# One pool of eight PSUM banks for a fused cross-attention and FFN layer: scores merged into three stretches a step

## The chip, the cores and the metric

The kernel runs on one core of a Trainium2 chip. The metric is device time in microseconds (us) of one launch. The engines are TensorE (PE), VectorE (DVE), ScalarE (ACT), GpSimd (POOL) and SyncE (SP), which issues the DMAs.

## The reference

For 32 batches of 224 tokens (`x`, width 512) and 750 context rows (width 384), a gated cross-attention is followed by a gated feed-forward network whose two linear layers are quantised:

```python
x = x + tanh(g_xattn) * attention(layernorm(x), ctx, mask, Wq, Wkv)     # 16 heads of 32
x = x + tanh(g_ffn)   * ffn(layernorm(x), w1, b1, w2, b2)               # 512 -> 2048 -> 512
# attention: q = x Wq^T, (k, v) = ctx Wkv^T; where(mask, q k^T / sqrt(32), -1e9); softmax; times v
# ffn: two layers, each on rmsnorm'ed tokens rounded to 8 bits with one scale a token and ternary weights;
#      an exact gelu lies between them
```

## The kernel before, in words

Attention is worked in 128 **steps**: 32 batches times 4 groups of 4 heads (`steps`). Four heads of width 32 fill the 128 rows of TensorE. In a step `n` the kernel does two things with scores.

- `maxima(b, g, i)`, for `i` in 0 to 2, computes the scores of step `n + 1` in the layout tokens by keys (matmuls `sm`, 112 rows) and DVE takes row maxima of them (`mx<-sm`). After `i == 2`, `minus_max` splits the negated maximum into three bf16 parts (six small DVE reductions), and `turn_max` turns them on TensorE (`pn`), with an ACT copy to `nT`.
- `weights(b, g, u)`, for `u` in 0 to 2, computes the scores of step `n` in the layout keys by tokens (matmuls `se`: first `nT` against ones, then keys against queries), and ACT takes `Exp` of all 1792 columns in one instruction (`p<-se`). POOL adds the results up into `acc`.

Both kinds of scores use one PSUM tile of four banks (`ps_s`, one buffer), in turn. Each step so has six **slots**: an even slot begins with `maxima` of the next step, an odd slot with `weights` of this step.

After the scores of a slot come **fillers**, which are matmul groups with an eviction each: `pk` (keys, evicted by ACT to `kT`), `pv` (values, by ACT or DVE to `v`), `pq` (queries, by DVE to `qT`), `pn`, `values` and `sums` (the weighted sums `po`, turned out by DVE to `oT`), and of the FFN `ph` (first layer, by DVE to `h`) and `po2` (second layer, `po` in the profile, by DVE to `xg`). Every filler takes a tile of its own from `ps_m`, a pool of four buffers of one bank each, so that a matmul waits only for the eviction of the filler that was four before it.

The order on each engine is the order of the program text (`Ordered` keeps it), and the framework puts in the semaphore waits, from the tiles that instructions write and read. `put(k, us, fn)` assigns a unit to a slot; units marked `first` come before the FFN's. `Ffn.fill` then draws FFN units as long as their estimated PE, ACT and DVE time fits the slot's room (`PE_ROOM`, less what is assigned), and the slot's other units follow. `Ffn.drain` writes out what is left after the last step, by a list of estimated durations. In the first steps `weight_units` quantises the FFN weights.

The names of the profile's groups are tiles: `sm` and `se` are scores, `p` the exponentials, and all instructions carry line 53, the line of the recording helper.

## Time and profile before

| | |
|---|---|
| three runs | 2985.87, 2986.15, 2988.3 us; median 2986.15 |
| span of the profiled execution, first to last instruction | 2983.6 us; its own time lies about 2.5 us above by the median run |
| PE busy | 2892.7 us (97%) |
| DVE, ACT, POOL busy | 1737.2, 1414.2, 2084.4 us (58%, 47%, 70%) |
| mean granted TensorE clock | 0.993 |
| HBM | 119.74 MB read, 29.27 MB written |
| first `se` matmul, first `se` of the last step, end | 32.9, 2894.9, 2983.6 us |

The profile has no separate time for the profiled execution beside its span, so the median run is set beside the span. The page gives busy shares and a chain of the work that ended last; the answers of the trace give groups of instructions, waits, a timeline in order of time, and windows. PE's rows are matmuls, PEld's the weight loads that run beside them. Ends of matmuls are modelled, so starts are the safer reading.

### The profile page before, as it was taken

How to read it: one execution, taken by the hardware profiler on the slowest of the kernel's cores; microseconds unless marked ns; L12 is line 12 of the kernel's file. 1: busy time of each engine (PE TensorE's matmuls, PEld its weight loads, DVE VectorE, ACT ScalarE, POOL GpSimd, SP SyncE). 2: the span in 40 equal slices, each digit the busy share in tenths (PEclk: the TensorE clock that was granted, in tenths of full speed). 3: DMA queues.
4: the chain of work that ended last, by engine and by line, in shares of the span. 5: the costliest groups of instructions: out<-in, count | busy, mean ns of one | idle time of the engine just before them, and what ended most of it. 6: DMA issues, size and time to landing. Idle time of an engine off the chain costs nothing.

```text
span 2983.6 us, 62984 instructions
## 1 busy us (share of the span) xinstructions
PE 2892.7 (97%) x26814; PEld 1840.7 (62%) x26814; DVE 1737.2 (58%) x2616; ACT 1414.2 (47%) x1438; POOL 2084.4 (70%) x2723
## 2 busy tenths in 40 slices
PE   8999999999999999999999999999999999999985
PEld 5666566666666666666666666666666666666653
DVE  5566555555556565555555565655655655556556
ACT  2344454544545455445445454544544554545444
POOL 3566767767766876777667777767767777777675
PEclk9999999999999999999999999999999999999998
DMA  5433222223222222222232212123122132222123
GB/s 148 106 99 98 55 50 73 43 62 75 42 61 61 52 55 73 69 44 48 63 73 47 65 40 80 48 62 74 45 50 62 45 71 67 50 71 48 39 52 78
DMA packets 375785, 189.80 MB, mean 64 GB/s; under 512 B 282160, under 2 KB 339920, under 8 KB 375376
## 3 DMA queue, kind: packets, MB, share of 16 engines
q1 hardware_dynamic: 375504, 185.79, 25.6%
q8 instruction: 209, 3.42, 0.5%
q14 instruction: 72, 0.59, 0.1%
HBM read 119.74 MB, written 29.27 MB: 50 GB/s over the span
## 4 chain that ended last, share of the span: by engine, by line
PE 82%; ACT 10%; POOL 3%; DVE 2%; issue 1%; DMA 1%; POOLq 0%; SPq 0%; ACTq 0%; DVEq 0%
PE po L53 17%; PE pk L53 15%; PE se L53 14%; PE sm L53 13%; PE pv_None L53 8%; ACT p L53 7%; PE pv L53 6%; PE ph L53 6%; PE pq L53 3%; DVE mx L53 2%; ACT L53 2%; POOL acc L53 1%; ACT h L53 1%; PE pn L53 1%; POOL h L53 1%
## 5 line engine op out<-in xcount | busy, mean ns | idle before, releaser
L53 POOL TENSOR_TENSOR acc<-acc,p 125x896 f32<-125x896 f32 x510 | 1066.9, 2092 | 324.8 <-ACT p L53 303.6
L53 DVE TENSOR_REDUCE mx<-sm 112x4 f32<-112x2000 f32 (+1 forms) x384 | 861.2, 2243 | 669.3 <-PE sm L53 669.2
L53 ACT ACTIVATE p<-se 125x1792 f32<-125x1792 f32 x384 | 638.8, 1663 | 760.6 <-PE se L53 706.9
L53 PE MATMUL pk<-y,wkv_sb 128*128 128x375 f32 x1536 | 541.6, 488 | 1.5 <-DMA y<-in_ctxT 1.5
L53 PE MATMUL sm<-kT,qT 32*112 32x500 f32 (+1 forms) x4096 | 426.9, 508 | 31.6 <-ACT p L53 22.7
L53 POOL TENSOR_TENSOR acc<-p 125x896 f32<-125x896 f32 x128 | 268.3, 2096 | 240.3 <-ACT p L53 237.1
L53 PEld LDWEIGHTS pk<-y,wkv_sb 128*128 128x128 f32 x1536 | 279.2, 190 | 175.7 <-issue 36.9
L53 PE MATMUL se<-qT,kT 32*125 32x224 f32 x6144 | 359.9, 348 | 0.0
L53 PE MATMUL po<-p,v 125*32 125x224 f32 x6144 | 317.1, 354 | 0.0
L53 PE MATMUL pv<-wkv_sb,y 128*125 128x256 f32 x1248 | 311.0, 385 | 0.0
L53 PEld LDWEIGHTS se<-qT,kT 32*125 32x125 f32 x6144 | 295.4, 183 | 0.1
L53 PEld LDWEIGHTS sm<-kT,qT 32*112 32x112 f32 x4096 | 159.3, 170 | 190.6 <-ACT p L53 137.6
L53 PEld LDWEIGHTS po<-p,v 125*32 125x32 f32 x6144 | 186.5, 110 | 118.9 <-issue 43.1
L53 PEld LDWEIGHTS pv<-wkv_sb,y 128*125 128x125 f32 x1248 | 223.3, 188 | 52.3 <-issue 17.8
L53 ACT COPY kT<-pk 128x375 f32<-128x375 f32 x256 | 120.1, 469 | 282.0 <-PE pk L53 281.2
L53 PE MATMUL pv_None<-wkv_sb,y 128*125 128x256 f32 x1056 | 250.9, 387 | 0.0
L53 PEld LDWEIGHTS pv_None<-wkv_sb,y 128*125 128x125 f32 x1056 | 191.3, 187 | 88.9 <-issue 59.7
L53 PE MATMUL po<-w2q,hT 128*128 128x256 fp8e4 x1792 | 220.9, 279 | 20.8 <-DMA hT<-hq 20.7
L53 DVE SCALAR_TENSOR_TENSOR h<-ph,qa_am,b_sb 128x512 f32<-128x512 f32 x216 | 158.5, 745 | 137.8 <-PE ph L53 110.3
L53 PE MATMUL ph<-w1q,xT 128*128 128x512 fp8e4 x896 | 224.9, 382 | 6.5 <-DMA xT<-xc 4.2
L53 PE MATMUL pq<-xTb,wq_sb 128*128 128x224 f32 x1024 | 221.4, 359 | 0.4 <-DVE wq_sb L53 0.4
L53 PEld LDWEIGHTS <-hT 128*128 128x128 bf16 x1792 | 171.5, 100 | 72.3 <-issue 27.1
(147 smaller groups left out, 2875.1 us busy)
## 6 DMA issues: line engine op xcount, KB each, us to landing
y<-in_ctxT SPq DMA_DIRECT2D x90, 375.0 KB, 4.4
x<-in_x SPq DMA_DIRECT2D x32, 448.0 KB, 4.1
xTb<-in_xT SPq DMA_DIRECT2D x32, 448.0 KB, 3.7
o_d<-yo SPq DMA_DIRECT2D x508, 28.0 KB, 1.8
xg<-in_x SPq DMA_DIRECT2D x26, 512.0 KB, 3.7
og<-o_d SPq DMA_DIRECT2D x26, 512.0 KB, 4.4
out<-xg SPq DMA_DIRECT2D x52, 256.0 KB, 2.1
wa<-in_w1T SPq DMA_DIRECT2D x8, 512.0 KB, 3.8
```

Source lines behind the costliest of these rows:

```text
L53: return lambda *args, **kw: tc.keep_in_program_order(build(*args, **kw))
```

## The change

The two pools in PSUM become two tiles of four banks, `s_lo` and `s_hi`. `weights` always writes `s_lo` and `maxima` always `s_hi`. The fillers take banks of these same tiles from `bank()`: after `take_banks(LOW + HIGH, HIGH)` the first four fillers of a stretch get the banks of `s_lo` in order, and further ones those of `s_hi`.

A step has three stretches: `weights`, at once `maxima`, then the fillers of two of the old slots. The maxima run a stretch ahead: the first third of step `n + 2` is already done in the last stretch of step `n`, and `turn_max` of step `n + 1` there too. The weighted sums of the step before move from slot 2 to the end of slot 1, the second `pk` from slot 1 to slot 2, and the `pq` of `g > 1` are put before the `pv` of their slots. The exponential is taken in two instructions of two banks each. The rooms for FFN units are set anew.

```diff
-    ps_s = pool("ps_s", 1, PSUM)
-    ps_m = pool("ps_m", 4, PSUM)
+    ps = pool("ps", 1, PSUM)
+    NB = 8
+    LOW, HIGH = list(range(NB // 2)), list(range(NB // 2, NB))
+    s_lo = ps.tile([P, NB // 2, 512], F32, name="s_lo")
+    s_hi = ps.tile([P, NB // 2, 512], F32, name="s_hi")
+    turn_of = {"order": LOW, "again": LOW, "at": 0}
+    def take_banks(order, again):
+        turn_of.update(order=order, again=again, at=0)
+    def bank():
+        n, order, again = turn_of["at"], turn_of["order"], turn_of["again"]
+        turn_of["at"] += 1
+        i = order[n] if n < len(order) else again[(n - len(order)) % len(again)]
+        return (s_lo if i < NB // 2 else s_hi)[:, i % (NB // 2), :]
...
-            pk = ps_m.tile([P, 512], F32, tag="m", name=f"pk_{b}_{g}_{half}")
+            pk = bank()
...
-        s = ps_s.tile([P, HG, 512], F32, tag="s", name=f"sm_{b}_{g}_{i}")
+        s = s_hi
...
-        s = ps_s.tile([P, HG, 512], F32, tag="s", name=f"se_{b}_{g}_{u}")
+        s = s_lo
...
-        act.activation(p.rearrange("p j i n -> p j (i n)"), s[:KC, :, : 2 * S], AF.Exp)
+        for two in (slice(0, HG // 2), slice(HG // 2, HG)):
+            act.activation(
+                p[:, two].rearrange("p j i n -> p j (i n)"), s[:KC, two, : 2 * S], AF.Exp
+            )
...
-    PE_ROOM = 2.5, 1.9
+    PE_ROOM = 5.2, 3.0
...
-        put(0, 0.2, lambda: turn_max(n), first=True)
+        put(4, 0.2, lambda: turn_max(n + 1), first=True)
         if last:
-            put(2, 2.7, lambda: (values(*last), sums(*last)), first=True)
-            put(5, 0.0, lambda: store(*last), first=True)
+            put(4, 0.0, lambda: store(*last), first=True)
...
+        if last:
+            put(1, 2.9, lambda: (values(*last), sums(*last)))
         for k in range(6):
             if k % 2 == 0:
-                maxima(*nxt, k // 2)
-            else:
-                if k == 3 and last:
+                take_banks(LOW + HIGH, HIGH)
+                if k == 2 and last:
                     finish(*last)
                 weights(b, g, k // 2)
-            if k == 4:
-                minus_max(n + 1)
+                at, i = ahead[k // 2]
+                if at < N:
+                    maxima(*steps[at], i)
+                if i == 2:
+                    minus_max(at)
+                room = PE_ROOM[0] - sum(us for us, _ in slots[k] + slots[k + 1])
...
+    take_banks(HIGH, HIGH)
     last = steps[-2:]
```

Here `ahead = [(n + 1, 1), (n + 1, 2), (n + 2, 0)]`.

More of the change, by code (lines that the diff above doesn't have):

```diff
@@ L209, in centre @@
     def centre(lo, hi):
-        pw = ps_m.tile([P, 512], F32, tag="m", name=f"pwq_{lo}")
+        pw = bank()
         for c in range(NDC):
@@ L246, in spread @@
             if b == 0:
-                pr = ps_m.tile([P, NQ, CP], F32, tag="m", name="prb")
+                pr = bank()[:, : NQ * CP].rearrange("p (t n) -> p t n", t=NQ)
                 for t in range(NQ):
@@ L262, in q_piece @@
         def q_piece(g, between=None):
-            pq = ps_m.tile([P, 512], F32, tag="m", name=f"pq_{b}_{g}")
+            pq = bank()
             for c in range(NDC):
@@ L297, in v_piece @@
         cols = slice(D + hv * D // 2, D + (hv + 1) * D // 2)
-        pv = ps_m.tile([P, 2, D // 2], F32, tag="m", name=f"pv_{b}_{hv}_{i}_{only}")
+        pv = bank().rearrange("p (a n) -> p a n", a=2)
         part = slice(0, 2) if only is None else slice(only, only + 1)
@@ L370, in turn_max @@
         b, g = steps[n]
-        pn = ps_m.tile([P, NQ, CP], BF16, tag="m", name=f"pn_{b}_{g}")
+        pn = bank().bitcast(BF16)[:, : NQ * CP].rearrange("p (t n) -> p t n", t=NQ)
         for t in range(NQ):
@@ L413, in values @@
     def values(b, g):
-        po = ps_m.tile([P, 512], F32, tag="m", name=f"po_{b}_{g}")
+        po = bank()
         po_of[b, g] = po
@@ L526, in mean @@
         def mean():
-            pm = ps_m.tile([P, 512], F32, tag="m", name="pwm")
+            pm = bank()
             pe.matmul(pm[:, 0:2], ones, tot, start=True, stop=True)
-            held["pm"] = pm
-        def scales():
-            pm = held.pop("pm")
             dve.tensor_scalar(wmean, pm[:, 0:2], 1.0 / (D * F), 1e-5, ALU.mult, ALU.max)
@@ L562, in two @@
                     fetch(*every[n + 1], "wb")
-                if n == 0:
-                    scales()
                 quantise(*wi)
@@ L784, in b_matmul @@
             cols = slice(f * 512, (f + 1) * 512)
-            ph = ps_m.tile([P, 512], F32, tag="m", name=f"ph_{i}_{t}_{f}")
+            ph = bank()
             for k in range(NDC):
@@ L842, in c_matmul @@
             cols = slice(half * D // 2, (half + 1) * D // 2)
-            po = ps_m.tile([P, D // 2], F32, tag="m", name=f"po2_{i}_{t}_{half}")
+            po = bank()[:, : D // 2]
             for k in range(NFC):
@@ L931, in flamingo_gated_layer @@
         "c": [[("PE", 1.75), ("DVE", 0.5)]], "out": [[("SP", 2.0)]],
-        "top": [[("PE", 0.3), ("ACT", 0.4)]],
         "w": [[("PE", 1.1), ("ACT", 1.7)]],
@@ L950, in flamingo_gated_layer @@
         for name, after in {
-            "w0": "top", "w1": "w0", "w2": "w1", "val": "", "fin0": "val", "sto0": "fin0",
+            "w0": "", "w1": "w0", "w2": "w1", "val": "", "fin0": "val", "sto0": "fin0",
             "vlast": "w2 val fin0", "fin1": "vlast fin0", "fin2": "vlast fin0",
@@ L1011, in fill @@
         def fill(self, rooms, stored, newest=False):
-            rooms, some = list(rooms), False
+            rooms, spent = list(rooms), 0.0
             rooms[0] += self.late(stored, 0 if rooms[0] >= 0.3 else 2)
@@ L1037, in fill @@
                 unit[6]()
-                some |= unit[3] > 0
+                spent += unit[3]
                 rooms = [room - us for us, room in zip(unit[3:6], rooms)]
@@ L1041, in fill @@
             self.slot += 1
-            return some
+            return spent
         def late(self, stored, more):
@@ L1147, in flamingo_gated_layer @@
     for i in range(WAKE):
-        wake = ps_m.tile([P, 512], F32, tag="m", name=f"wake_{i}")
+        wake = bank()
         pe.matmul(wake, idle[:, :P], idle, start=True, stop=True)
@@ L1183, in flamingo_gated_layer @@
     first_k[0]()
+    maxima(*steps[1], 0)
+    turn_max(0)
     ffn = Ffn()
@@ L1194, in flamingo_gated_layer @@
         b, g = steps[n]
-        nxt = steps[n + 1]
+        ahead = [(n + 1, 1), (n + 1, 2), (n + 2, 0)]
         last = steps[n - 1] if 0 < n else None
@@ L1219, in flamingo_gated_layer @@
                 put(0, 1.9, ks[0])
-            put(1, 1.9, ks[1])
+            put(2, 1.9, ks[1])
         if g == 2 and b + 2 < B:
@@ L1229, in flamingo_gated_layer @@
         if n == 0:
-            put(3, 1.7, lambda: centre(2 * P, D))
+            put(1, 1.7, lambda: centre(2 * P, D))
         if n < 2:
-            put(5, 1.5, q0[n + 2])
+            put(3, 1.5, q0[n + 2])
+        more = b + 1 < B
+        if more and g > 1:
+            put(3, 1.5, qs[2 * g - 4])
+            put(5, 1.5, qs[2 * g - 3])
         lent = v_left[0] if v_left else None
@@ L1237, in flamingo_gated_layer @@
             put_values(3, 5)
-        more = b + 1 < B
         if more and g == 0:
@@ L1246, in flamingo_gated_layer @@
             put(5, 0.0, lambda: load_xT(b + 1))
-        if more and g > 1:
-            put(3, 1.5, qs[2 * g - 4])
-            put(5, 1.5, qs[2 * g - 3])
+        if last:
+            put(1, 2.9, lambda: (values(*last), sums(*last)))
         for k in range(6):
             if k % 2 == 0:
-                maxima(*nxt, k // 2)
-            else:
-                if k == 3 and last:
+                take_banks(LOW + HIGH, HIGH)
+                if k == 2 and last:
                     finish(*last)
                 weights(b, g, k // 2)
-            if k == 4:
-                minus_max(n + 1)
-            used = sum(us for us, _ in slots[k])
+                at, i = ahead[k // 2]
[4 more added lines that the diff above has]
+                room = PE_ROOM[0] - sum(us for us, _ in slots[k] + slots[k + 1])
             early = [unit for us, unit in slots[k] if unit in quick]
@@ L1264, in flamingo_gated_layer @@
             if wunits:
-                if k in (1, 3, 5):
+                if k % 2:
                     wunits.pop(0)()
@@ L1268, in flamingo_gated_layer @@
                 ffn.closing = n == N - 2 and k > 2
-                some = ffn.fill(
-                    (PE_ROOM[k % 2] - used, (1.1, 2.2)[k % 2], 1.7),
-                    (n - (k < 5)) // NG if n else 0,
-                )
-                if k == 0 and not some and lent is not None:
+                spent = ffn.fill(
+                    (min(room, PE_ROOM[1]), (2.2, 1.3)[k % 2], 1.7),
+                    (n - (k < 4)) // NG if n else 0,
+                )
+                room -= spent
+                if k == 0 and not spent and lent is not None:
                     v_piece(*lent, 0)
@@ L1282, in flamingo_gated_layer @@
                     unit()
+    take_banks(HIGH, HIGH)
     last = steps[-2:]
     ffn.drain(
-        [("top", 0, None, 0, 0, 0, lambda: turn_max(N - 1))]
-        + [(f"w{u}", 0, None, 0, 0, 0, lambda u=u: weights(*last[1], u)) for u in range(3)]
+        [(f"w{u}", 0, None, 0, 0, 0, lambda u=u: weights(*last[1], u)) for u in range(3)]
         + [
```

## The prediction

> **What bounds the kernel now.** I read the page's busy and clock lines first, then the chain, then the waits, then one stretch of the timeline, and last the rows of the evictions.

> ```profile
> PE 2892.7 (97%) x26814; PEld 1840.7 (62%) x26814; DVE 1737.2 (58%) x2616; ACT 1414.2 (47%) x1438; POOL 2084.4 (70%) x2723
> ...
> PE 82%; ACT 10%; POOL 3%; DVE 2%; issue 1%; DMA 1%; POOLq 0%; SPq 0%; ACTq 0%; DVEq 0%
> ```

> PE is busy for 97% of the span, and 82% of the chain is PE. To check that this busy time is real, I took starts of successive matmul groups from 60 to 2855 us and compared each distance with the usual one of its pair of kinds: the excess is 127 us, 17 of it jitter inside a `se` group. So waits cost PE 110 us in the loop. That is all that any reordering can win.

> ```profile
> PEld sm L53 <- ACT p L53: 137.6, 247, 2.5
> ...
> PEld L53 <- DVE mx L53: 28.9, 41, 2.8
> ```

> The waits name the chief cause: `sm` waits for the exponentials, since both scores share a tile. One such place:

> ```profile
> 1510.50 0.93 PE L53 MATMUL se<-qT,kT 32*125 32x224 f32 x16
> ...
> 1511.35 1.56 PE L53 MATMUL pv<-wkv_sb,y 128*125 128x256 f32 x6
> 1511.56 1.66 ACT L53 ACTIVATE p<-se 125x1792 f32<-125x1792 f32 x1 [0.61 <-PE se L53]
> ...
> 1512.95 0.42 DVE L53 COPY v<-pv 125x256 f32<-125x256 f32 x1 [1.76 <-PE pv L53]
> ...
> 1513.28 1.11 PE L53 MATMUL sm<-kT,qT 32*112 32x500 f32 x8 [0.36 <-ACT p L53]
> ```

> `se` frees PE after 0.86 us, `p` starts 0.20 later, and `sm` starts 0.05 after `p` ends. The filler `pv` covers all but 0.36 of it. The half `pv` itself frees PE after 1.39 us (1512.74); its copy starts 0.21 later, the next group in between unhindered. This independence of a filler from its eviction is what the change touches.

> **What the change moves.** The diff suggests bank by bank sharing. The built program's order, with its waits, shows another thing: all waits go by the tile, and a tile is now four banks. In program order of the changed kernel, a whole stretch reads:

> ```
> 5037 L53 Matmult s_lo<-qT_10707,kT_2_11567 125x224 x8
> 5038 L53 Matmult s_hi<-kT_3_11775,qT_10707 112x250 x8
> 5039 L53 Matmult s_lo<-wkv_sb,y_11171 125x256 [waits DMAHW7_49,Activation_49]
> 5041 L53 Matmult s_lo<-y_11171,wkv_sb 128x375 [waits Activation_49]
> 5043 L53 Matmult s_lo<-p_1_0_11788,v_0_11050 32x224 [waits Activation_49]
> 5047 L53 Matmult s_lo<-acc_1_11791,ones 32x224 [waits Pool_49]
> 5050 L53 Matmult s_lo<-nT_2_11941,ones_143 125x448 [waits DVE_49]
> ```

> I followed the semaphore counts. Row 5039 waits for the second half of the exponential, though its bank is in the first half. Row 5041, another bank, waits for the copy of 5039's result; 5043 for the copy of 5041's; 5050 for the transposition of `po`. Over the 381 stretches there are 1278 fillers: 380 first ones wait for the whole exponential, 841 later ones for the eviction of the filler just before, and 376 `se` groups for that of the last filler. In the 59 stretches whose last filler lies in `s_hi`, the `se` wait is on an older one, so it is hidden. That leaves 841 + 376 - 59 = 1158 exposed evictions. TensorE's order is fixed, so behind each waiting matmul the whole rest of PE's queue stands, and ACT, DVE and POOL behind that.

> **Terms.** (1) The old stalls go: -110 us.

> (2) First fillers. The rows of `v` give ACT's price from PSUM:

> ```profile
> L53 ACT COPY v<-pv 125x256 f32<-125x256 f32 x122 | 45.2, 370 | 144.3 <-PE pv L53 144.0
> ...
> L53 ACT COPY v<-pv_None 125x512 f32<-125x512 f32 x67 | 39.1, 584 | 207.7 <-PE pv_None L53 207.7
> ```

> 214 ns for 256 columns more is 0.836 ns a column and 0.156 us fixed, so half an exponential (896 columns) takes 0.90 us and both 1.81 (1.66 unsplit; at most 2.0). The first filler starts 0.20 + 1.81 + 0.05 = 2.06 us after `se`, and `maxima` covers 1.04 of that. 380 x 1.02 = +388 us (bounds 330 to 450).

> (3) Evictions. Each costs its start lag (0.11 to 0.21 us in the timeline), its duration and 0.05:

> ```profile
> L53 ACT COPY kT<-pk 128x375 f32<-128x375 f32 x256 | 120.1, 469 | 282.0 <-PE pk L53 281.2
> ...
> L53 DVE SCALAR_TENSOR_TENSOR h<-ph,qa_am,b_sb 128x512 f32<-128x512 f32 x216 | 158.5, 745 | 137.8 <-PE ph L53 110.3
> ...
> L53 DVE STREAM_TRANSPOSE oT<-po 128x448 f32<-128x448 f32 x128 | 83.2, 650 | 76.5 <-PE po L53 70.2 <-POOL r_m L53 3.7 <-POOL r_a L53 1.8
> ```

> By count in the waits: `kT` 251 at 0.63, `h` 208 at 1.00, `v` on ACT 207 at 0.55 and on DVE 98 at 0.58, `nT` 126 at 0.60 (341 ns row), `xg` 101 at 0.73 (478 ns), `qT` 93 at 0.55 (389 ns), `oT` 126 at 0.90: 851 us for 1210, 0.70 each. For 1158 it is +814 us (10% either way: 730 to 900).

> (4) Queues. Evictions now stand on PE's path, and so does what their engine has queued before them. I walked nine successive stretches of the changed order by hand with row durations. The plain one of rows 5037 on: 0.24 + 0.86 + 2.06 to the first filler, then `pv` 1.39 + 0.53, `pk` 1.98 + 0.63, `values` and `sums` 2.78 + 0.90: 11.4 us. A stretch with `gelu` behind the exponential: two table loads of 1.28, gelu 1.91 and warm 0.20 hold ACT for 4.67 us, from 3.13 to 7.80; `pk` is through at 5.16, its copy is not before 8.27: 2.5 us lost. Six others lose 0.45 to 0.62 or nothing to `Square`, to the rounding, or to `mx` (2.24 us) with `minus_max` (1.2) on DVE. Nine stretches: 98.8 us, 5.1 of it queues, so 1.7 us a step; 127 x 1.7 = +218 us (bounds 0 and twice that). The walk without queues, 31.2 us a step, agrees with (1) to (3): 22.54 - 0.87 + 3.05 + 6.41 = 31.1.

> (5) Ends. Drain has as many `po2` (12) and 16 `ph` instead of 22, all in `s_hi` and each behind the last eviction: about 16 x 0.9 + 6 x 0.7, less 6 x 0.87 for the `ph` no longer there: +14 us, and +6 in the start.

> The other moves cost nothing that I can see: `sums` comes after its `acc` with a stretch to spare, as before; `turn_max` lies a stretch ahead of its use; 384 more ACT starts are in (2). On SP, `store` is queued one slot earlier, ahead of the loads of that slot, four issues in 2.65 us by the timeline's row: a load behind them lands that much later, and its data is first read a stretch of some 10 us on; without that cover it is 2.65 us a step, 337 in all.

> Sum at full clock: 2983.6 - 110 + 388 + 814 + 218 + 20 = 4314 us.

> (6) The clock. PE would be busy some 65% of the time, in pieces. What the profile shows of that:

> ```profile
> 2862.30:2865.70 3.40, 1.11 (x8) 0.42 (x9) 1.09 (x1) 2.97 (x2) 2.16 (x2) 1.00 0.00 0
> 2865.70:2869.10 3.40, 2.13 (x20) 1.51 (x19) 2.23 (x7) 0.00 (x0) 3.40 (x2) 0.50 0.85 159
> 2869.10:2872.50 3.40, 1.62 (x8) 0.46 (x8) 1.64 (x4) 1.66 (x1) 3.13 (x7) 0.50 0.20 29
> ```

> Columns: window, length, busy PE, PEld, DVE, ACT, POOL, clock, DMA. After 3.4 us with 1.11 busy, the clock was halved, and it stayed so until a nearly full window at 2872.5. Windows of the drain that I count 40 to 46% filled by their matmuls' lengths kept it. The gelu stretches have an idle time of 3.2 us, and some that begin with `ph` reach 2.5. I count 50 falls, each half-speed for about 10 us with PE 80% busy: 4 us each, +200 us (40 to 550: from 10 falls to 140).

> [...]

> Forecast: 4314 + 200 = 4514 us, and 2.5 us between span and run: 4517 us. Low: all but (1) to (3) gone and (6) at 40: 4116. High: queues doubled and (6) at 550: 5082.

> **Rivals.** *Not slower:* the waits are there but already over when PE comes to them. It needs less than 110 / 1538 = 0.07 us for each of 380 + 1158 waits; then the time is 2984 - 110 = 2874 and up. Against it: lag and release alone are 0.16 to 0.26 us. 3%.

> *Sharing acts bank by bank:* only the last filler's eviction stands before `se` (321 x 0.76 = 244 us), and the first filler needs only half the exponential (380 x 0.11 = 42): 2984 - 110 + 286 = 3160 us. For it: the diff. Against it: the counts in the program's waits. [...] 6%.

> *The clock stays down:* after a fall no window gets full, since each filler is followed by 0.7 us idle. At a mean clock of 0.75, the 2750 us of PE work take 917 more, less some 190 as a slow `maxima` covers the exponential: 5040 us; at 0.65 about 5600. Decided by whether `se`, `sm` and a filler on end refill a window; at half speed they last 7 us, so mostly yes. 14%.

> My forecast has 77%. The range 4110 to 5090 holds it and a third of the last rival. A measurement of this kernel can tell about 0.2%, 6 us, from no change: faster 0.03, same 0.01, slower 0.96.

> **What would show it.** Right: PE near 65% busy; idle before `pk`, `pv` and `po` released by ACT and DVE, some 1500 times and 0.7 to 1 us each; `p` in 768 rows of about 0.90 us; the chain shared among PE, ACT and DVE; half-clock windows beside gelu. Wrong: fillers that start before the eviction ahead of them has ended, or a step under 28 us.

## The result, and the profile after

The changed kernel takes 4569.25 us (median of four runs, 4551.65 to 4576.48), against 2986.01 us for the kernel before beside it: ratio 1.530, 95% interval 1.527 to 1.533. Its profiled execution has a span of 4565.8 us and a mean granted clock of 0.927 (before 0.993). From its page, the busy times of the engines and the shares of the chain that ended last:

```profile
PE 3233.1 (71%) x26814; PEld 2034.1 (45%) x26814; DVE 1767.7 (39%) x2603; ACT 1458.0 (32%) x1868; POOL 2097.8 (46%) x2735
...
PE 58%; ACT 19%; DVE 16%; issue 4%; POOL 2%; DMA 0%; DVEq 0%; ACTq 0%; POOLq 0%
```

The same 26814 matmuls keep PE busy for 71% of the span, not 97%. ACT and DVE together have 35% of the chain, where they had 12%, though their busy time grew by only 44 and 31 us: it is not their work that grew, it has come onto the path. The waits of PE (us in total, times, longest; a row `A <- B` is the time that A waited for B), in the order of the answer:

```profile
PE s_lo L53 <- ACT p L53: 378.4, 383, 4.3
...
PE s_lo L53 <- DVE h L53: 243.5, 187, 2.6
...
PE s_lo L53 <- ACT v L53: 160.9, 202, 3.4
PE s_lo L53 <- ACT kT L53: 152.6, 254, 2.9
...
PE s_lo L53 <- DVE oT L53: 106.6, 126, 0.9
...
PE s_lo L53 <- DVE v L53: 60.8, 81, 1.8
...
PE s_lo L53 <- ACT nT L53: 55.2, 127, 0.4
PE s_lo L53 <- DVE xg L53: 52.8, 72, 1.1
PE s_lo L53 <- DVE qT L53: 52.6, 93, 1.5
```

The first row is the first filler of a stretch behind the exponential: 383 times, 0.99 us each. The eight others are evictions of the filler just before: 1142 times, 885 us, 0.78 each. Before, the largest such row was that of the weight loads of `sm` behind the exponential, 247 times and 137.6 us in all. Per instruction the engines do what they did: a copy to `kT` takes 472 ns on average (before 469), and half an exponential 914 ns:

```profile
L53 ACT ACTIVATE p<-s_lo 125x896 f32<-125x896 f32 x768 | 662.6, 914 | 1615.6 <-PE s_lo L53 1581.1 <-POOL r_a L53 13.1 <-POOL r_y L53 11.5
```

One whole stretch, in order of time. The brackets say how long the engine was idle, and who ended that:

```profile
2295.85 0.41 PE L53 MATMUL s_lo<-nT,ones 3*125 3x448 bf16 x4 [0.84 <-DVE oT L53]
...
2296.79 1.06 PE L53 MATMUL s_hi<-kT,qT 32*112 32x500 f32 x8
2297.08 1.73 ACT L53 ACTIVATE p<-s_lo 125x896 f32<-125x896 f32 x2 [6.92 <-PE s_lo L53]
2297.92 2.24 DVE L53 TENSOR_REDUCE mx<-s_hi 112x4 f32<-112x2000 f32 x1 [1.89 <-PE s_hi L53]
...
2298.85 1.02 PE L53 MATMUL s_lo<-w1q,xT 128*128 128x512 fp8e4 x4 [1.00 <-ACT p L53]
...
2301.34 0.74 DVE L53 SCALAR_TENSOR_TENSOR h<-s_lo,qa_am,b_sb 128x512 f32<-128x512 f32 x1
...
2302.14 4.12 PE L53 MATMUL s_lo<-y,wkv_sb 128*128 128x375 f32 x6 [2.26 <-DVE h L53]
...
2306.29 0.47 ACT L53 COPY kT<-s_lo 128x375 f32<-128x375 f32 x1 [7.49 <-PE s_lo L53]
...
2306.82 2.92 PE L53 MATMUL s_lo<-wkv_sb,y 128*125 128x256 f32 x6 [0.56 <-ACT kT L53]
...
2309.84 0.42 DVE L53 COPY v<-s_lo 125x256 f32<-125x256 f32 x1 [7.69 <-PE s_lo L53]
2310.32 0.64 PE L53 MATMUL s_lo<-nT,ones 3*125 3x448 bf16 x4 [0.58 <-DVE v L53]
```

The filler at 2298.85 (`ph`) starts 0.04 us after both halves of the exponential. Its own eviction `h` could have started at 2299.9, but DVE is still in `mx` and then in the six reductions of `minus_max`, so `pk` starts 2.26 us after PE went idle, though it writes another bank. `pv` waits for the copy of `pk`, the next scores for the copy of `pv`. That `pk` takes 4.12 us and not 2.06 (the median of its 256 groups in the kernel before) shows the second cost, the clock. The windows round its fall (window, length, busy PE, PEld, DVE, ACT, POOL, granted clock, DMA share, GB/s):

```profile
2294.16:2297.58 3.42, 2.58 (x48) 1.61 (x40) 0.85 (x2) 0.50 (x1) 0.56 (x1) 1.00 0.01 3
2297.58:2300.99 3.41, 1.29 (x8) 0.38 (x4) 2.94 (x5) 1.22 (x2) 2.08 (x1) 1.00 0.54 110
2300.99:2304.40 3.41, 2.26 (x4) 1.40 (x5) 1.10 (x5) 0.00 (x0) 2.07 (x1) 0.50 0.16 57
```

One window with 1.29 us of matmuls in 3.41, and from 2300.99 the clock is half, here for 13.65 us. There are 96 such falls on record, the last of them after the last instruction, and 666 us at half clock; before there were 8, and 45 us.

Counted start to start, as in the prediction, from 33 us to the last four steps, the distances between matmul groups exceed the usual ones by 1372 us at full clock and 262 at half (before: 103 and 4). That is 1527 of the 1582 us between the spans. The other 55 lie in the start and in the drain, which runs partly at half clock (61 us of the last 101).

### The profile page after: what moved, and what is told of

The parts are those of the page before. It is cut to its first block, busy times and chain, and to the rows that moved or that the text cites. A ratio compares the mean times of both kernels' runs of the same rounds, so it can differ in the third digit from the quotient of the medians.

```text
span 4565.8 us, 64142 instructions
## 1 busy us (share of the span) xinstructions
PE 3233.1 (71%) x26814; PEld 2034.1 (45%) x26814; DVE 1767.7 (39%) x2603; ACT 1458.0 (32%) x1868; POOL 2097.8 (46%) x2735
## 4 chain that ended last, share of the span: by engine, by line
PE 58%; ACT 19%; DVE 16%; issue 4%; POOL 2%; DMA 0%; DVEq 0%; ACTq 0%; POOLq 0%
PE s_lo L53 52%; ACT p L53 10%; PE s_hi L53 6%; DVE mx L53 5%; DVE h L53 3%; ACT kT L53 2%; DVE oT L53 2%; ACT L53 2%; ACT v L53 2%; ACT h L53 1%; ACT hq L53 1%; POOL acc L53 1%; DVE qT L53 1%; DVE xg L53 1%; DVE st L53 1%
## 5 line engine op out<-in xcount | busy, mean ns | idle before, releaser
L53 POOL TENSOR_TENSOR acc<-acc,p 125x896 f32<-125x896 f32 x510 | 1068.7, 2095 | 928.6 <-ACT p L53 908.6
L53 DVE TENSOR_REDUCE mx<-s_hi 112x4 f32<-112x2000 f32 (+1 forms) x384 | 861.1, 2243 | 1022.7 <-PE s_hi L53 1022.6
L53 ACT ACTIVATE p<-s_lo 125x896 f32<-125x896 f32 x768 | 662.6, 914 | 1615.6 <-PE s_lo L53 1581.1
L53 PE MATMUL s_lo<-y,wkv_sb 128*128 128x375 f32 x1536 | 660.6, 574 | 285.2 <-DVE h L53 98.6
L53 PE MATMUL s_lo<-wkv_sb,y 128*125 128x256 f32 x2154 | 597.3, 421 | 240.8 <-ACT p L53 75.6
L53 PEld LDWEIGHTS s_lo<-wkv_sb,y 128*125 128x125 f32 x2154 | 407.6, 201 | 428.6 <-ACT p L53 110.8
L53 PEld LDWEIGHTS s_lo<-y,wkv_sb 128*128 128x128 f32 x1536 | 313.5, 218 | 602.6 <-ACT p L53 162.8
L53 POOL TENSOR_TENSOR acc<-p 125x896 f32<-125x896 f32 x128 | 273.8, 2139 | 641.4 <-ACT p L53 641.4
L53 PE MATMUL s_hi<-kT,qT 32*112 32x500 f32 (+1 forms) x4096 | 429.4, 498 | 1.7 <-DVE qT L53 0.9
L53 ACT COPY kT<-s_lo 128x375 f32<-128x375 f32 x256 | 120.7, 472 | 862.2 <-PE s_lo L53 862.2
L53 PE MATMUL s_lo<-qT,kT 32*125 32x224 f32 x6144 | 395.3, 363 | 0.0
L53 POOL TENSOR_TENSOR yo<-oT,rd 128x224 f32<-128x224 f32 x127 | 71.5, 563 | 680.3 <-DVE rd L53 680.3
L53 PE MATMUL s_lo<-p,v 125*32 125x224 f32 x6048 | 319.5, 360 | 84.1 <-ACT kT L53 57.3
L53 PE MATMUL s_lo<-w1q,xT 128*128 128x512 fp8e4 x800 | 221.8, 402 | 201.8 <-DVE h L53 97.4
L53 DVE STREAM_TRANSPOSE oT<-s_lo 128x448 f32<-128x448 f32 x126 | 81.9, 650 | 647.6 <-PE s_lo L53 646.3
L53 PEld LDWEIGHTS s_lo<-qT,kT 32*125 32x125 f32 x6144 | 325.1, 192 | 0.0
L53 PE MATMUL s_lo<-nT,ones 3*125 3x448 bf16 x1536 | 163.2, 403 | 224.7 <-DVE oT L53 106.6
L53 PEld LDWEIGHTS s_lo<-p,v 125*32 125x32 f32 x6048 | 184.9, 112 | 248.2 <-ACT kT L53 129.3
L53 PEld LDWEIGHTS <-xT 128*128 128x128 bf16 x896 | 91.1, 102 | 382.4 <-issue 313.5
L53 PEld LDWEIGHTS <-ones 3*125 3x125 bf16 x1536 | 96.2, 132 | 339.0 <-issue 338.8
L53 PEld LDWEIGHTS <-hT 128*128 128x128 bf16 x1792 | 179.2, 100 | 142.3 <-issue 102.1
L53 PE MATMUL s_lo<-w2q,hT 128*128 128x256 fp8e4 x1616 | 195.9, 275 | 65.4 <-DVE xg L53 21.9
## 6 DMA issues: line engine op xcount, KB each, us to landing
og<-o_d SPq DMA_DIRECT2D x26, 512.0 KB, 11.4
```

What stands on the lines that cost most here:

```text
L53: return lambda *args, **kw: tc.keep_in_program_order(build(*args, **kw))
```

## The experiments

The theory was the prediction's: waits go by the tile, so with a tile of four banks a filler is no longer independent of the filler before it. The rivals were that the new order costs the time (scores in pairs, maxima a stretch ahead, the exponential in two), that ACT's long instructions do, or that the clock does.

"Stalls" below are the excess at full clock, start to start, in the loop, and depend by some tens of us on what is taken as usual; "half clock" is over the whole profiled run.

| kernel | time, us | ratio to before, 95% | stalls, us | falls, half clock us |
|---|---|---|---|---|
| before | 2983.4 | 1 | 103 | 8, 45 |
| after | 4569.25 | 1.527–1.533 | 1372 | 96, 666 |
| one_tile | 3909.70 | 1.308–1.313 | 830 | 86, 461 |
| alternate | 3812.63 | 1.277–1.282 | 799 | 62, 266 |
| two_tiles | 3540.93 | 1.185–1.189 | 549 | 39, 188 |
| four_tiles | 3147.72 | 1.054–1.057 | 200 | 21, 97 |
| eight_tiles | 3016.88 | 1.010–1.013 | 64 | 25, 125 |
| no_gelu | 4462.50 | 1.494–1.502 | 1305 | 76, 613 |
| one_exp | 4546.58 | 1.522–1.526 | 1346 | 88, 647 |
| before_split | 2979.84 | 0.9980–0.9998 | 100 | 7, 44 |
| before_halves | 2980.91 | 0.9983–1.0001 | 104 | 8, 48 |

**one_tile: the old order, only the pool of fillers changed.** The kernel before, with its four filler banks as one tile, taken in turn.

```diff
-    ps_m = pool("ps_m", 4, PSUM)
+    ps_m = pool("ps_m", 1, PSUM)
+    s_m = ps_m.tile([P, 4, 512], F32, name="s_m")
...
-            pk = ps_m.tile([P, 512], F32, tag="m", name=f"pk_{b}_{g}_{half}")
+            pk = bank()          # s_m[:, turn % 4, :]
```

> The kernel before, in its own order, with one edit: the fillers no longer have four tiles of one bank each, but take the four banks of one tile in turn. Theory (a wait goes by the tile, so a filler waits for the eviction of the one before): by the program's waits 508 fillers stand directly behind the eviction of the filler before them (213 of h at 1.0 us, 126 of nT at 0.6, 103 of xg at 0.73, the rest v), 387 us, and 380 more have a group of scores between, which hides it; with queues 0 to 150 us: 3370 to 3530 us. Rival (sharing acts by the bank, the new order is what costs): 2986 us within 1%.

It took 3909.70 us, 926 more than before, with not an instruction moved. The sign is the theory's, the size is not: the expectation priced each wait at an idle engine's eviction. Waits of one_tile:

```profile
PE s_m L53 <- DVE h L53: 273.8, 212, 5.5
...
PE s_m L53 <- ACT nT L53: 113.4, 126, 3.7
```

`h` costs 1.29 us a time and `nT` 0.90, where lag, duration and release alone are 1.00 and 0.60. In the timeline most of these evictions find their engine free; the rest stand in its queue. Of 214 `h`, 35 start late behind `mx` or the reductions of `minus_max`, and 33 behind other work on DVE; of 128 `nT`, 20 stand behind a table load and its `warm` on ACT, and start 2.8 us after their matmuls. And the 86 falls had not been priced.

**two_tiles, four_tiles, eight_tiles: the new order, tiles cut smaller.** First `s_lo` as two tiles of two banks, fillers alternating between them; then `s_hi` too, with the row maxima in two instructions; then eight tiles of one bank, exponential and maxima in four instructions each, and only two banks of `s_lo` used by fillers. The fillers' banks are so chosen anew each time.

```diff
-    s_lo = ps.tile([P, NB // 2, 512], F32, name="s_lo")
+    s_lo = [ps.tile([P, 2, 512], F32, name=f"s_lo{i}") for i in range(2)]      # two_tiles, four_tiles
-    LOW, HIGH = list(range(NB // 2)), list(range(NB // 2, NB))
+    LOW, HIGH = [0, 2, 1, 3], list(range(NB // 2, NB))                         # two_tiles
+    LOW, HIGH = [0, 2], [4, 6, 5, 7]            # four_tiles, with s_hi as two tiles
...
+    s_lo = [ps.tile([P, 512], F32, name=f"s_lo{i}") for i in range(NB // 2)]   # eight_tiles, and s_hi
+    LOW, HIGH = [0], list(range(NB // 2, NB))                                  # eight_tiles, as what follows
...
+                take_banks(LOW + HIGH, [1] + HIGH)
-        put(4, 0.2, lambda: turn_max(n + 1), first=True)
+        put(4, 0.2, lambda: turn_max(n + 1))     # no longer first: behind FFN units and values of its slot
```

> The changed kernel with s_lo as two tiles of two banks, one for each half of the exponential, and the fillers' banks in the order 0, 2, 1, 3, so that successive fillers lie in different tiles. Nothing else is changed. Theory: the second and later fillers no longer wait, the first waits for half an exponential (0.11 us), the last filler's eviction still stands before the next scores (321 x 0.76 us): 2984 - 110 + 42 + 244 = 3160 us, with queues and the clock 3150 to 3320. Rival (the clock or the stretches' order makes the loss): above 4000 us.

> As two_tiles, and s_hi as two tiles as well, the row maxima taken in two instructions, and the fillers of a stretch in the banks 0, 2, 4, 6, 5, 7: from the third on they lie in the tiles of the maxima, so that the next scores by keys find their banks free, and an eviction of the last filler is hidden by the matmuls of those scores. Theory: only the 60 or so stretches with two fillers pay a last eviction (41 us) and the first fillers 42 us, less the 110 us of old waits: 2960 us, with queues up to 3040. Rival (the order of stretches is itself worse than the six slots): over 3100 us.

> The changed kernel with eight tiles of one bank: the exponential and the row maxima in four instructions each, the first filler of a stretch in bank 0, the next ones in 4 to 7, and pn behind the other fillers of its slot. Theory: with waits by the bank nearly nothing is exposed; the first filler needs one quarter of the exponential (0.53 us, hidden by the maxima's matmuls), the last filler's eviction is hidden by the next scores. 2984 - 110 and 50 to 150 us for ACT queues behind gelu: 2920 to 3030 us. Rival (four_tiles lost its 160 us to the longer queues of ACT and DVE, which more instructions make worse): above 3150 us.

Each cut brings the time down, and with a bank to a tile 1552 of the 1586 us that the change cost are back, while scores in pairs, maxima ahead, moved sums and the rooms stay (the turn of the maxima stands later in its slot). So the order as a whole is not what costs. The starts show where the wait ends: at full clock the first filler begins 0.05 us after the second half of the exponential in the changed kernel (350 stretches), and 0.05 us after the first half in two_tiles and four_tiles (726). The two in between missed their ranges by 221 and 108 us. In two_tiles the same waits remain and are dearer than expected: PE waits 115 us for the exponential (42 expected) and 373 us for evictions (244 expected), and 188 us are at half clock. In four_tiles the largest row of PE is:

```profile
PE s_lo L53 <- ACT p L53: 129.0, 388, 3.3
```

So 388 first fillers still wait for half an exponential, 0.33 us each on average where 0.11 was expected (at full clock the median is 0.17). In eight_tiles, where a quarter is enough, the row is down to 3.6 us; one of its stretches:

```profile
2304.66 1.85 ACT L53 ACTIVATE p<-s_lo 125x448 f32<-125x448 f32 x4 [4.89 <-PE s_lo L53]
2305.40 1.56 PE L53 MATMUL s_lo<-wkv_sb,y 128*125 128x256 f32 x6
...
2306.80 0.26 PE L53 MATMUL s_hi<-identb,nb 112*128 112x112 bf16 x2
2306.90 1.74 PE L53 MATMUL s_hi<-xTb,wq_sb 128*128 128x224 f32 x8
2307.00 0.37 ACT L53 COPY v<-s_lo 125x256 f32<-125x256 f32 x1 [0.49 <-PE s_lo L53]
```

`pv` starts while the exponential is running, and two further groups start before its copy does. The stalls of eight_tiles come out at 64 us by the count above, but PE is idle for 166 us by its page, against 91 in the kernel before, so that they are below those of before is not shown. It is 1.2% slower: it is 29 us behind by the 16th step, 9 of them already at the first `se`. The clock was at half for 41 us of the first 400 (before: 7), which can account for 17 us at most. And a wait for `nT` has grown (before: 5.0 us, 12 times), perhaps because its turn stands later, which no run tested:

```profile
PE s_lo L53 <- ACT nT L53: 62.2, 39, 4.2
```

**alternate: the tiles left, only the order of banks changed.** Successive fillers take `s_lo` and `s_hi` by turns.

```diff
-                take_banks(LOW + HIGH, HIGH)
+                take_banks([i for two in zip(LOW, HIGH) for i in two], HIGH)
```

> The changed kernel with its two tiles of four banks, but the fillers' banks in the order 0, 4, 1, 5, 2, 6, 3, 7, so that successive fillers lie in different tiles. One line. Theory: a filler then waits for the eviction of the one before the last, which the last one's matmuls hide; the first still waits for the exponential (360 us), the second for the row maxima (short ones pay: about 190), and some 234 last fillers in s_lo stand before the next scores (175): 2984 - 110 + 360 + 190 + 175, with queues and the clock 200 to 400 as the other variants showed: 3800 to 4000 us. The pairs of ph that follow each other no longer leave two idle gaps in a window of the clock, so falls of the clock go from 96 to under 50. Rival (the tile does not matter): 4569 us, 96 falls.

One line takes 757 us off. The time is in the expected range; the falls are not (62, not under 50). Its waits:

```profile
PE s_lo L53 <- ACT p L53: 402.0, 382, 4.3
...
PE s_hi L53 <- DVE mx L53: 159.5, 197, 2.1
```

A filler now waits for the one two before it, which is mostly over. The first filler waits as it did, and the second meets a new wait, for `mx` in `s_hi`.

**no_gelu: the queue and the clock.** The gelu is left out (identity in its place), so there are no table loads.

```diff
-            act.activation(h, h, AF.Gelu)
+            act.activation(h, h, AF.Identity)
```

> The changed kernel with the identity in place of gelu (this leaves the gelu out), so that ACT loads no tables in the loop. Theory of the prediction: the ACT time before an eviction falls from 4.67 to 1.9 us 54 times, some 2.5 us of PE's path each (135 us), and with those long gaps most falls of the clock go (about half of the 333 us of half-speed loss at most): 4569 - 135 - 60 to 170, so 4260 to 4380 us, mean clock 0.95 or more. Rival (falls come from the ordinary gaps behind the exponential and short fillers): clock still 0.93, 4430 us.

It took 4462.50 us, 107 off, outside the theory's range and nearer to the rival's 4430. The profiled execution is the slowest of its four, 4486.01 us at a clock of 0.932: in it stalls fell by 67 us, half of the 135 expected, the time at half clock by 53, and 74 of 95 falls remain. The other three had a clock of 0.940, which is some 535 us at half clock (2 x 0.060 x 4461), so without the gelu usually some 130 us of it go. Long instructions on ACT are neither the main part of the stalls nor the place of most falls.

**one_exp: the exponential in one instruction again.**

```diff
-        for two in (slice(0, HG // 2), slice(HG // 2, HG)):
-            act.activation(
-                p[:, two].rearrange("p j i n -> p j (i n)"), s[:KC, two, : 2 * S], AF.Exp
-            )
+        act.activation(p.rearrange("p j i n -> p j (i n)"), s[:KC, :, : 2 * S], AF.Exp)
```

> The changed kernel with the exponential in one instruction again. Theory (the first filler waits for the whole exponential whatever its halves, so the split only adds its fixed part to PE's path): 380 x 0.15 = 57 us less by the prediction's 1.81 us for both halves; by the changed kernel's own trace, where both halves take 1.73 us, 380 x 0.07 = 27 us less. So 4510 to 4545 us. Rival (the first half frees the first filler): one instruction is then slower, by up to 380 x 0.8 = 300 us.

It took 4546.58 us: 23 us off, 1.6 us above its range. From the first start to the last end the exponential takes 1.66 us in place of 1.73, and the first filler again begins 0.05 us after it. The split costs its fixed part and wins nothing as long as both halves share a tile.

**before_split, before_halves: what points to a faster version.** The kernel before, with the scores' tile as two of two banks, exponential and maxima in two instructions; in the second, `sm` also does heads 0 and 1 first, then 2 and 3.

```diff
-        s = ps_s.tile([P, HG, 512], F32, tag="s", name=f"sm_{b}_{g}_{i}")
+        s = [ps_s.tile([P, 2, 512], F32, tag=f"s{w}", name=f"sm{w}_{b}_{g}_{i}") for w in range(2)]
-        for t, lo, hi, col in TAKES[i]:
-            for j in range(HG):
+        for two in (range(HG // 2), range(HG // 2, HG)):                            # before_halves
+            for t, lo, hi, col, j in [(*take, j) for take in TAKES[i] for j in two]:
...
```

> The kernel before in its own order, with the four banks of scores as two tiles of two banks; exponential and row maxima in two instructions each (both of 768 in place of 384). Theory (the wait goes by the tile, so a second tile hands the first half on earlier): in the kernel before `sm` waits 0.56 us each time for the exponential (137.6 us over 247). The first two matmuls of `sm` now need only its first half, which ends some 0.7 us earlier; the second half ends 0.15 us later than the one instruction did (1.81 against 1.66), and the first two matmuls, 0.28 us of work, are done by then: 0.13 us less at 247 places, so 2984 - 32 = 2952 us, from 2930 to 2975. Rival (the four heads run beside each other on TensorE, so two of them done earlier win nothing, and the later end of the exponential and the fixed parts of 768 more instructions are paid): 2984 + 0.15 x 250 to 380 = 3021 to 3040 us.

> As before_split, and the matmuls of `sm` go by halves too: heads 0 and 1 for both runs of tokens, then heads 2 and 3. Theory: the first half of `sm` (0.55 us) lies beside the second half of the exponential, so of 0.56 + 0.15 us of wait some 0.55 go: 2984 - 0.41 x 247 = 2883 us at best, 2890 to 2950. Rival (TensorE works on the four heads at once, and with two at a time `sm` of 8 matmuls, 1.11 us, becomes longer, up to twice): up to 256 + 0 ... 384 x 1.0 us more, 3050 to 3400 us.

Neither side's numbers came. before_split's interval just excludes no change (some 4 us less), that of before_halves does not. before_halves shows why so little is won, at the same place as the prediction's stretch of before:

```profile
1508.44 1.56 PE L53 MATMUL pv<-wkv_sb,y 128*125 128x256 f32 x6
1508.62 1.73 ACT L53 ACTIVATE p<-se 125x896 f32<-125x896 f32 x2 [0.58 <-PE se L53]
...
1509.93 1.55 PE L53 MATMUL sm<-kT,qT 32*112 32x500 f32 x8
...
1510.39 0.27 PEld L53 LDWEIGHTS sm<-kT,qT 32*112 32x112 f32 x4 [0.19 <-ACT p L53]
...
1511.42 0.27 PE L53 MATMUL pn<-identb,nb 112*128 112x112 bf16 x2
```

In the kernel before, `pn` follows at:

```profile
1514.32 0.27 PE L53 MATMUL pn<-identb,nb 112*128 112x112 bf16 x2
```

`sm` starts 1.49 us after `pv`, not 1.93, but its second half waits for the second half of the exponential, and `pn` starts 2.98 us after `pv`, as before (2.97). In all, the distances between matmuls inside `sm` grew by 37 us. The starts of the single matmuls say why the head start is lost. In the kernel before, the four heads of an `sm` of 8 matmuls start within 0.02 us, their second matmuls 0.51 us later, and the next group at 1.04 us: the heads run beside each other. In the stretch above, heads 0 and 1 start their first and second matmuls at 1509.93 and 1510.44, heads 2 and 3 at 1510.39 and 1510.90, and `pn` starts 1.03 us after 1510.39. Two heads took as long as four (1.03 and 1.04 us to the next group), so what counted was when the last two could start, and two of them done earlier won nothing, as the rival of before_split said. The losses that the rivals added did not come: both halves of the exponential take 1.73 us against 1.66, and where nothing waits the pairs overlap (the median `sm` of 8 still takes 1.04 us). No version here beats the kernel before by more than 0.2%.

## Why the prediction was right, and where not

The forecast was 4517 us; the time is 4569.

- **Waits by the tile** (steps 2 and 3). Right, and shown by one_tile, alternate and the three cuts. First fillers: 383 waits, 378 us, against 380 and 388. Evictions: 1142 waits against 1158.
- **Evictions and queues** (steps 3 and 4). 814 and 218 were forecast, 1032; the start-to-start count gives 1372 less the first fillers' 358 in that count, 1014 (the rows above have 885, but they count from the modelled ends of matmuls, which lie later than PE is free for the next group: an `sm` of 8 is drawn 1.11 us long in the kernel before, and the next group starts 1.04 us after its first matmul). How it parts was only sketched by nine stretches: gelu stretches were to be some 106 us of the 218 (2.5 of 9 x 127 / 3), and no_gelu's stalls fell by 67. `mx` with `minus_max` on DVE, taken at 0.45 to 0.62 us or nothing, cost 1.36 ahead of `h` in the stretch above, and 35 of the 216 `h` start behind these reductions, 1.46 us after their matmuls on average. The two errors have opposite signs, so that the sum came within 2% is in part luck.
- **Old waits** (step 1). They went: 110 forecast, 103 in this count.
- **Ends** (step 5). 20 forecast, some 55 found, which include half-clock time in the drain.
- **The clock** (step 6). 262 us in the loop against 200, within its bounds, but by luck of two factors: 95 falls in the run and not 50, 6.9 us each at half clock and not 10. The place was wrong. Only 32 of the 95 lie near a table load. In 36 the widest gap of PE is between two `ph`, in 24 between a `ph` and a `pk`: `ph` is short and its eviction long (1.02 us of PE, then 1.3 of waiting on average by the row of `h`, 2.26 in the stretch above), so two waits round one `ph` leave a window mostly empty.
- **Rivals.** Bank by bank (3160) did not come; kernels with smaller tiles come near it or below (four_tiles 3148, eight_tiles 3017), with other banks for their fillers. "The clock stays down" (5040) did not come: it rose again after two windows on average. The first rival needed waits already over; 1525 were not.

No long gap stands beside most falls: the one at 2300.99 has none over 2.26 us, and in 81 of the 95 no gap that touches the window before is as long as the window, 3.41 us. Short ones are many: beside the 1525 waits above, 0.83 us each on average, stand 96 falls against 8.

What stays open: which edit of the changed order, if any one, accounts for the 33 us of eight_tiles over before, and exactly how full a window must be to bring the clock back.

## What to carry to other kernels

Count the tiles and not the banks: in these kernels the waits went by the tile that the framework guards, so a ring of buffers had to be a ring of tiles (four banks as one tile cost 926 us in one_tile; a bank to a tile took back 1552 of 1586 in eight_tiles). When buffers are merged, price every eviction together with what its engine has queued ahead of it, and then ask what the pieces leave of the clock (666 us at half clock here, 45 before). If the tiles can't be changed, choose the order of banks so that neighbours in time lie in different tiles: one line gave 757 us.

## What the runs showed of the hardware

The number of falls did not follow the total of stalls: alternate and one_tile have almost the same stalls (799 and 830 us) and 62 against 86 falls, 266 against 461 us at half clock. That it depends on how the stalls lie together is an estimate from the windows above; no run moved stalls alone to test it.

The four heads of an `sm` ran beside each other: in the kernel before, their first matmuls (32 rows each) started within 0.02 us, and the next group 1.04 us after the first; in before_halves the last two heads alone took 1.03 us to the next group.
